# Edge loop of a graph layer: one head of the values weighed by ScalarE, and the softmax's maximum and sum taken into the exponential

## The chip, the cores and the metric

The kernel runs on one core of a Trainium2 chip. The metric is the device time of one execution in microseconds (us). Before the change three runs gave 2769.37, 2779.38 and 2781.32 us, with a median of 2779.38. Engines are named as in the profile: PE (TensorE, matmuls; PEld is its weight load), DVE (VectorE), ACT (ScalarE), POOL (GpSimd) and SP (SyncE, which issues DMAs). Each engine works through its own queue in order; engines wait for one another by semaphores.

## The reference, cut to what matters

There are 3125 nodes with 256 features and 103125 directed edges (each node has a self-loop). A graph layer, a linear-attention mixer and a mixture of experts follow one another. The change is in the graph layer, in the attention over edges. With `H = 4` heads of `DK = 56`:

```python
att = jnp.einsum('ehd,ed->eh', k, q.sum(axis=1)) / SQRT_DK
v = jnp.concatenate([Vn, ek], axis=1).reshape(-1, H, DK)

def seg_softmax(att, idx, n):
    m = jax.ops.segment_max(att, idx, num_segments=n)
    e = jnp.exp(att - m[idx])
    s = jax.ops.segment_sum(e, idx, num_segments=n)
    return e / (s[idx] + 1e-16)

res = (v * att[:, :, None]).reshape(-1, H * DK)
agg = jax.ops.segment_sum(res, col, num_segments=n) + jax.ops.segment_sum(res_i, row, num_segments=n)
```

It is computed for both directions of every edge. A node's value is 192 features of its own (three heads of 56 and 24 features of the fourth head) followed by 32 features made of the edge's time.

## The kernel before, in words

The nodes are sorted by their number of edges and cut into 25 blocks of 128 nodes, one node to a partition. A block has as many *slots* as its busiest node has edges: 60 in the first block that is worked on, then 44, 42, 40 and so on down to 22, 854 in all. The work is cut further into 118 *chunks* of six to eight slots. All blocks with their chunks are worked on in `edge_blocks` (L1203 to L1491), in an order that is written out by hand (`tc.manual_schedule`, L1435); nothing is reordered by a planner. The loop over the chunks `q` issues, on every engine's queue in this order:

- `gather(q + 3)`: POOL fetches one row of the node table per slot (L357).
- `first_times(q)`: PE adds up one group of time features (L1340).
- `take` (L1417) on ACT, for the block that ended three chunks ago.
- If the chunk before was the last of its block ("over"), `softmax_exp` of that block: ACT's exponential (L1376), all eight columns (two directions, four heads) at once.
- `find(q + 1)`: DVE picks each slot's record (L1305, L1306) and forms part of the logits (L1310, L1311). It needs `compare(q + 1)`.
- `angles(q + 1)`: PE transposes the times that find left (L1317, tile pt); ACT copies them out (L1319, tile turned, called lT in the code) and copies the gathered values into the tile keep (L1322); then ACT runs `compare(q + 2)` (one L1295 per slot, and L1296); then PE multiplies by the frequencies (L1326) and ACT takes sines and squares, three times (L1328, L1329).
- If over: `softmax_two` of that block on DVE (L1382 to L1392: sum, reciprocal, scaling, and the two directions added into the tile both), and then `weigh` for each of its chunks. In weigh DVE multiplies three heads of the values by their weights (L1400), the 24 features of the fourth (L1402) and the time features (L1404), and PE adds the slots up in PSUM with one matmul by the identity per slot (L1406, two passes each in float32).
- `logits(q)` on DVE (L1349 to L1357), which needs the sines and squares of `angles(q)`.
- `finish` for a block that ended three chunks ago, and at the end of a block `sums` and `softmax_one` (L1412 to L1414 and L1363 to L1372: add the parts, take the maximum over the slots, subtract it).

Two consequences of in-order queues matter. On PE, the transpose of `angles(q + 2)` stands behind the whole burst of L1406 that a block boundary issues. On ACT, `compare(q + 3)` stands behind the copy of that transpose. The tile keep has nine buffers; the gathered rows have four.

A second path for other graphs (`edge_tiles`, called at L858) is skipped at run time unless a check of the fast path fails.

Of the kernel before, what the change touches and what calls it, by code (L numbers as in the profile page):

```python
# [10 lines left out]
F32 = mybir.dt.float32  # L11
I32 = mybir.dt.int32
AF = mybir.ActivationFunctionType
OP = mybir.AluOpType
AX = mybir.AxisListType
# [3 lines left out]
P = 128  # L19
D = 256  # L20
TD = 32
GH = 4
DK = (D - TD) // GH
# [43 lines left out]
def bc(ap, axis, n):  # L67

    u = ap.unsqueeze(axis)
    shape = list(u.shape)  # L70
    shape[axis] = n
    return u.to_broadcast(shape)
# [1130 lines left out]
def edge_blocks(tc, a, table, kept, abuf, slots, ordt, ord_i, counts, bad, ident, ones, scatter_rows, gather_rows,  # L1203
# [7 lines left out]
    nc = tc.nc  # L1211
# [3 lines left out]
    line = list(reversed(range(len(slots))))  # L1215
    for i in line:
        c = slots[i]
        k = -(-c // CHUNK)
# [3 lines left out]
    with ExitStack() as ctx:  # L1222
        one = ctx.enter_context(tc.tile_pool(name="e1", bufs=1))
        two = ctx.enter_context(tc.tile_pool(name="e2", bufs=2))
# [12 lines left out]
        for dst, k in ((w3, "w_time"), (b3, "b_time")):  # L1237
            s = a[f"L0_gnn_{k}"]
# [21 lines left out]
        blk, chk = {}, {}  # L1260
# [99 lines left out]
        def softmax_one(i):  # L1360
            c, b = slots[i], blk[i]
            att, shared = b["att"], b["shared"]
            nc.vector.tensor_tensor(shared[:, :c], shared[:, :c], bc(b["k"][:, :, 2], 2, GH), OP.add)  # L1363
            ah = att[:, :c, :6].rearrange("p s (d h) -> p s d h", d=2)
            nc.vector.tensor_tensor(ah, ah, bc(shared[:, :c, :3], 2, 2), OP.add)
            nc.vector.scalar_tensor_tensor(att[:, :c, 6:], att[:, :c, 6:], -2.0, bc(shared[:, :c, 3], 2, 2),
                                           op0=OP.mult, op1=OP.add)

            mx = two.tile([P, 2 * GH], F32, name="mx")
            nc.vector.tensor_reduce(mx, att[:, :c].rearrange("p s k -> p k s"), AX.X, OP.max)  # L1370
            nc.vector.tensor_scalar(mx, mx, 0.1 * NEG, None, op0=OP.max)
            nc.vector.tensor_tensor(att[:, :c], att[:, :c], bc(mx, 1, c), OP.subtract)  # L1372

        def softmax_exp(i):
            af = blk[i]["att"][:, :slots[i]]
            nc.scalar.activation(af, af, AF.Exp, scale=scale)  # L1376

        def softmax_two(i):
            c, b = slots[i], blk[i]
            att = b["att"]  # L1380
            sm = b["sm"] = two.tile([P, 2 * GH], F32, name="sm")
            nc.vector.tensor_reduce(sm, att[:, :c].rearrange("p s k -> p k s"), AX.X, OP.add)  # L1382
            rc = two.tile([P, 2 * GH], F32, name="rc")
            nc.vector.tensor_scalar(rc, sm, 1e-16, None, op0=OP.add)
            nc.vector.reciprocal(rc, rc)
            nc.vector.tensor_tensor(att[:, :c], att[:, :c], bc(rc, 1, c), OP.mult)
            both = b["both"] = two.tile([P, CAP, GH], F32, name="both")
            nc.vector.tensor_tensor(both[:, :c, :3], att[:, :c, :3], att[:, :c, 3:6], OP.add)
            nc.vector.tensor_tensor(both[:, :c, 3], att[:, :c, 6], att[:, :c, 7], OP.add)

            nc.vector.tensor_tensor(sm, sm, rc, OP.mult)
            nc.vector.tensor_tensor(sm[:, 6:7], sm[:, 6:7], sm[:, 7:], OP.add)  # L1392

        def weigh(q):
            i, s0, s1 = chunks[q]
            n, c, b, keep = s1 - s0, slots[i], chk[q]["b"], chk[q]["keep"]
            if s0 == 0:
                b["pa"] = psa.tile([P, KEEP], F32, name="pa")
            v3 = keep[:, :n, :3 * DK].rearrange("p s (h e) -> p s h e", e=DK)
            nc.vector.tensor_tensor(v3, v3, bc(b["both"][:, s0:s1, :3], 3, DK), OP.mult)  # L1400
            v1 = keep[:, :n, 3 * DK:PROJ]
            nc.vector.tensor_tensor(v1, v1, bc(b["both"][:, s0:s1, 3], 2, TAILH), OP.mult)  # L1402
            vt = keep[:, :n, PROJ:].rearrange("p s (m j) -> p s m j", j=TD)
            nc.vector.tensor_tensor(vt, vt, bc(b["att"][:, s0:s1, 6:], 3, TD), OP.mult)  # L1404
            for s in range(n):
                nc.tensor.matmul(b["pa"], ident, keep[:, s, :], start=(s0 + s == 0), stop=(s0 + s == c - 1))  # L1406
# [24 lines left out]
        n = len(chunks)  # L1431
# [3 lines left out]
        with tc.manual_schedule():  # L1435
# [8 lines left out]
            for q in range(n):  # L1444
                i, s0, s1 = chunks[q]
# [6 lines left out]
                if over is not None:  # L1452
                    softmax_exp(over)
# [3 lines left out]
                if over is not None:  # L1457
                    softmax_two(over)
                    j0 = q - len(pieces[over])
                    for j in range(j0, q):  # L1460
                        weigh(j)
# [3 lines left out]
                if ends[q] is not None:  # L1465
                    sums(i)
                    softmax_one(i)
# [7 lines left out]
                if q == 4:  # L1475
                    between()
            softmax_exp(line[-1])
            for q in (n - 3, n - 2):
                if ends.get(q) is not None:
                    take(ends[q])  # L1480
                    finish(ends[q])
            softmax_two(line[-1])
            for j in range(n - len(pieces[line[-1]]), n):
                weigh(j)
# [172 lines left out]
```

## Time and profile before

| what | value |
|---|---|
| runs | 2769.37, 2779.38, 2781.32 us, median 2779.38 |
| profiled execution | 2770.56 us, its span 2768.9 us |
| mean granted TensorE clock | 0.703 of full speed |
| busy over the span | DVE 2089.2 us (75%), PE 1951.6 (70%), POOL 1485.0 (54%), ACT 1226.2 (44%) |
| block boundaries, 663 to 2106 us of the span | 1443 us: DVE 1406.8 busy, PE 1108.6, POOL 950.3, ACT 854.0 |
| what comes before and after the edge loop | 0 to 540 us: preparation and mixer; 2135 to 2769 us: the rest of the layer and the experts |

The three runs have a median 8.8 us above the profiled execution. The times between the first and the last instruction are the span; sums of durations below are set against the profiled execution. In lists by group the columns are: line, engine, operation, tiles, shapes and count; then busy us and mean ns of one; then the engine's idle time before these instructions, with what ended it. In a list of waits: who waited for whom, us in total, times, longest. In a timeline: start in us, length in us, engine, line, operation, count, and in brackets the idle time before it with what ended it. Matmuls are pipelined, so that a busy PE is not PE at its peak.

### The profile page before, as it was taken

The numbers are of one execution on the slowest core, as the hardware profiler recorded it, in microseconds if no ns is written. First come the engines' busy times: TensorE is split into PE (matmuls) and PEld (weight loads), VectorE is DVE, ScalarE is ACT, GpSimd is POOL, SyncE is SP. The second block draws the span as 40 slices with busy tenths as digits, with TensorE's granted clock in tenths as the row PEclk, the third lists the DMA queues.
The fourth block names the chain that finished last, engine by engine and source line by source line (L and its number), as shares of the span: only waits on it lengthen the run. The fifth ranks groups of instructions, "written<-read, shape, count | busy, mean of one in ns | idle before, by whom it ended". The sixth has DMA issues, their size and how long they took to land. (4 is left out here: it accounts for less than half of the span.)

```text
span 2768.9 us, 25919 instructions
## 1 busy us (share of the span) xinstructions
PE 1951.6 (70%) x6193; PEld 1210.2 (44%) x6193; DVE 2089.2 (75%) x3744; ACT 1226.2 (44%) x3019; POOL 1485.0 (54%) x1527
## 2 busy tenths in 40 slices
PE   1138567558777777777777778777775945499994
PEld 0014234424344444444544434444544633277773
DVE  5545667669999999999999999999995557122226
ACT  1101122355655556655566666566562333033332
POOL 2632665476767776666666777666560541522220
PEclk7559778856666666666666666766756865599997
DMA  9541563496766666655566666566563762355554
GB/s 284 190 125 52 185 202 117 150 383 193 204 179 183 182 185 183 190 171 167 167 180 191 193 191 182 171 182 191 152 191 124 254 194 86 130 169 175 171 162 143
DMA packets 233243, 493.03 MB, mean 178 GB/s; under 512 B 33573, under 2 KB 144452, under 8 KB 232452
## 3 DMA queue, kind: packets, MB, share of 16 engines
q0 software_dynamic: 88720, 327.84, 39.1%
q1 hardware_dynamic: 114916, 130.10, 15.0%
q10 hardware_dynamic: 29456, 33.42, 3.8%
q8 instruction: 54, 0.88, 0.1%
q14 instruction: 97, 0.79, 0.1%
HBM read 412.86 MB, written 78.37 MB: 177 GB/s over the span
## 5 line engine op out<-in xcount | busy, mean ns | idle before, releaser
L357 POOL DMA_INDIRECT rowt<-table,idx x854 | 971.8, 1138 | 466.4 <-issue 433.2
L1326 PE MATMUL ps_u<-wide,turned 49*128 49x448 f32 (+2 forms) x708 | 532.3, 913 | 43.5 <-ACT turned L1319 40.8
L1406 PE MATMUL pa<-keep,ident 128*128 128x256 f32 x1708 | 428.6, 418 | 17.9 <-DVE keep L1404 17.7
L1406 PEld LDWEIGHTS pa<-keep,ident 128*128 128x128 f32 x1708 | 360.6, 213 | 110.5 <-DVE keep L1404 39.9
L1340 PE MATMUL pe<-te,ident 128*128 128x256 f32 x472 | 202.3, 577 | 245.0 <-ACT te L1329 243.0
L1326 PEld LDWEIGHTS ps_u<-wide,turned 49*128 49x128 f32 x708 | 196.2, 296 | 285.3 <-issue 186.1
L1340 PEld LDWEIGHTS pe<-te,ident 128*128 128x128 f32 x472 | 128.6, 297 | 381.0 <-ACT te L1329 361.7
L1319 ACT COPY turned<-pt 42x128 f32<-42x128 f32 (+2 forms) x118 | 30.6, 259 | 571.5 <-PE pt L1317 571.5
L1357 DVE TENSOR_REDUCE att<-rowt 128x56 f32<-128x1792 f32 (+2 forms) x118 | 245.8, 2083 | 4.0
L1295 ACT ACTIVATE rowt<-rowt,KT 128x60 f32<-128x60 f32 x854 | 215.8, 334 | 17.6 <-DMA rowt<-table,idx 17.4
L1305 DVE TENSOR_TENSOR rowt<-rowt 128x1260 f32<-128x1260 f32 (+2 forms) x118 | 178.2, 1510 | 40.3 <-DMA rowt<-table,idx 25.5
L1354 DVE TENSOR_TENSOR rowt<-rowt,qq 128x672 f32<-128x672 f32 (+2 forms) x236 | 197.6, 878 | 4.0
L1129 ACT ACTIVATE hT<-ps_h,b 128x128 f32<-128x128 f32 x256 | 94.1, 368 | 236.3 <-PE ps_h L1128 236.1
L351 POOL DMA_INDIRECT ybuf<-y,to_i x64 | 61.5, 960 | 242.6 <-DVE y L1137 228.9
L1328 ACT ACTIVATE half<-ps_u 128x448 f32<-128x448 f32 (+2 forms) x354 | 190.8, 539 | 0.3
L1128 PE MATMUL ps_h<-zT,w 128*128 128x128 f32 x1024 | 179.9, 295 | 12.4 <-ACT hT L1129 9.9
L1306 DVE TENSOR_REDUCE KT<-rowt 128x21 f32<-128x1260 f32 (+2 forms) x118 | 178.3, 1511 | 4.1
L1128 PEld LDWEIGHTS ps_h<-zT,w 128*128 128x128 f32 x1024 | 150.1, 192 | 57.0 <-ACT hT L1129 44.8
L1400 DVE TENSOR_TENSOR keep<-keep,both 128x1176 f32<-128x1176 f32 (+2 forms) x118 | 167.0, 1416 | 0.0
L1322 ACT COPY keep<-rowt 128x1344 f32<-128x1344 f32 (+2 forms) x118 | 159.2, 1349 | 10.8 <-PE pa L1406 10.8
L1133 PE MATMUL ps_e<-w,hT 128*128 x512 | 157.4, 390 | 0.0
L722 PE MATMUL ps<-w,xT 128*128 x172 | 99.6, 716 | 63.5 <-ACT xT L286 63.5
(369 smaller groups left out, 3250.6 us busy)
## 6 DMA issues: line engine op xcount, KB each, us to landing
w<-in_L_ffn_w_dram SPq DMA_DIRECT2D x80, 512.0 KB, 3.6
rowt<-table,idx POOLq DMA_INDIRECT x854, 4.1
h<-in_L_gnn_Wa_dram SPq DMA_DIRECT2D x19, 512.0 KB, 4.4
zbuf<-zero SPq DMA_DIRECT2D x1, 8514.0 KB
zr<-zbuf SPq DMA_DIRECT2D x64, 129.0 KB
yb<-ybuf SPq DMA_DIRECT2D x16, 384.0 KB, 5.5
xbuf<-blank SPq DMA_DIRECT2D x1, 5654.0 KB
abuf<-zero SPq DMA_DIRECT2D x1, 5632.0 KB
```

The lines of the kernel that those rows point to most:

```text
L357: nc.gpsimd.indirect_dma_start(out=dst, out_offset=None, in_=buf[:, :], in_offset=IndirectOffsetOnAxis(ap=idx, axis=0))
L1128: nc.tensor.matmul(ps[:, f, :], w1[:, c, f * P:(f + 1) * P], zT[:, c, :], start=(c == 0), stop=(c == 1))
L1295: nc.scalar.activation(key[:, s, :], key[:, s, :], AF.Square, bias=chk[q]["b"]["k"][:, s0 + s, 1:2])
L1305: nc.vector.tensor_tensor(times, times, bc(rowt[:, :n, :CAP], 2, 3), OP.mult)
L1306: nc.vector.tensor_reduce(b["times"][:, s0:s1, 1::2], times, AX.X, OP.add)
L1326: nc.tensor.matmul(ps[:, :n * 2 * TD], lT, wide[:, k, :n * 2 * TD], start=True, stop=True)
L1328: nc.scalar.activation(half[:, :n, :].rearrange("p s j -> p (s j)"), ps[:, :n * 2 * TD], AF.Sin)
L1340: nc.tensor.matmul(pe[:, :e - s, :], ident, chk[q]["te"][:, 0, s:e, :], start=(s0 + s == 0), stop=(s0 + e == c))
L1354: nc.vector.tensor_tensor(to, kt, bc(qq[:, :n, d, :], 2, 3), OP.mult)
L1357: nc.vector.tensor_reduce(b["att"][:, s0:s1, :], rowt[:, :n, :8 * TD].rearrange("p s (k j) -> p s k j", j=TD), AX.X, OP.add)
L1400: nc.vector.tensor_tensor(v3, v3, bc(b["both"][:, s0:s1, :3], 3, DK), OP.mult)
L1406: nc.tensor.matmul(b["pa"], ident, keep[:, s, :], start=(s0 + s == 0), stop=(s0 + s == c - 1))
```

## The change

Three things are changed, all in `edge_blocks`.

1. `softmax_one` no longer subtracts the maximum from the logits. It computes `low = -scale * maximum`, eight numbers per node.
2. `softmax_exp` runs one exponential per column (eight instead of one), with that column of `low` as bias, and has each deliver the sum over the slots as by-product into `sm`. `softmax_two` no longer computes the sum.
3. In `weigh`, for every block but the first, ACT multiplies the first head's 56 features slot by slot, with the weight as a scale per partition; DVE multiplies the second and third head only. The first block is weighed by DVE as before.

```diff
@@ softmax_one
             nc.vector.tensor_scalar(mx, mx, 0.1 * NEG, None, op0=OP.max)
-            nc.vector.tensor_tensor(att[:, :c], att[:, :c], bc(mx, 1, c), OP.subtract)
+            b["low"] = two.tile([P, 2 * GH], F32, name="low")
+            nc.vector.tensor_scalar(b["low"], mx, -scale, None, op0=OP.mult)
 
         def softmax_exp(i):
-            af = blk[i]["att"][:, :slots[i]]
-            nc.scalar.activation(af, af, AF.Exp, scale=scale)
+            b = blk[i]
+            sm = b["sm"] = two.tile([P, 2 * GH], F32, name="sm")
+            for k in range(2 * GH):
+                ak = b["att"][:, :slots[i], k]
+                nc.scalar.activation(ak, ak, AF.Exp, scale=scale, bias=b["low"][:, k:k + 1], accum_out=sm[:, k:k + 1])
 
         def softmax_two(i):
             c, b = slots[i], blk[i]
             att = b["att"]
-            sm = b["sm"] = two.tile([P, 2 * GH], F32, name="sm")
-            nc.vector.tensor_reduce(sm, att[:, :c].rearrange("p s k -> p k s"), AX.X, OP.add)
+            sm = b["sm"]
             rc = two.tile([P, 2 * GH], F32, name="rc")
@@ weigh
-            v3 = keep[:, :n, :3 * DK].rearrange("p s (h e) -> p s h e", e=DK)
-            nc.vector.tensor_tensor(v3, v3, bc(b["both"][:, s0:s1, :3], 3, DK), OP.mult)
+
+            h0 = 0 if i == line[0] else 1
+            for s in range(n * h0):
+                nc.scalar.activation(keep[:, s, :DK], keep[:, s, :DK], AF.Copy, scale=b["both"][:, s0 + s, 0:1])
+            vh = keep[:, :n, h0 * DK:3 * DK].rearrange("p s (h e) -> p s h e", e=DK)
+            nc.vector.tensor_tensor(vh, vh, bc(b["both"][:, s0:s1, h0:3], 3, DK), OP.mult)
```

Each matmul of weigh waits for the copy of its own slot. DVE's multiplications wait for none of the copies. The copies stand in ACT's queue behind `angles(q + 1)`, where weigh stands in the order above; the matmuls and their order are unchanged.

## The prediction

> **What bounds the kernel now.** First the windows view, cut at the edge loop, then its waits, then one block boundary in order of time. Its columns are busy us of PE, PEld, DVE, ACT, POOL, then the granted clock:
>
> ```profile
> 663.00:2106.00 1443.00, 1108.63 (x2863) 661.64 (x2863) 1406.80 (x1799) 854.04 (x2005) 950.33 (x817) 0.65 0.61 177
> ```
>
> VectorE is busy for 1406.8 of 1443 us, ScalarE for 854.0. By shares alone VectorE is the limit, and work taken from it is time won. The waits of the same stretch say more:
>
> ```profile
> ACT turned L1319 <- PE pt L1317: 550.2, 109, 19.1
> DVE rowt L1305 <- ACT rowt L1296: 5.0, 9, 1.2
> PE pa L1406 <- DVE keep L1404: 5.8, 14, 1.0
> ```
>
> ScalarE's idle time is one wait, for the transpose of L1317, up to 19.1 us at once; and VectorE's few stalls end with ScalarE's L1296. The boundary after the 40-slot block shows how they hang together (lines of the timeline):
>
> ```profile
> 896.41 0.47 ACT L1376 ACTIVATE att<-att 128x320 f32<-128x320 f32 x1
> ...
> 899.78 0.26 ACT L1319 COPY turned<-pt 48x128 f32<-48x128 f32 x1 [2.90 <-PE pt L1317]
> ...
> 903.63 0.16 DVE L1392 TENSOR_TENSOR sm<-sm 128x1 f32<-128x1 f32 x1
> ...
> 906.18 19.81 PE L1406 MATMUL pa<-keep,ident 128*128 128x256 f32 x80 [0.60 <-DVE keep L1404]
> ...
> 908.36 0.63 ACT L1329 ACTIVATE te<-half 128x512 f32<-128x512 f32 x1
> ...
> 926.69 0.27 PE L1317 MATMUL pt<-ident,KT 128*48 128x128 f32 x1
> 927.00 0.26 ACT L1319 COPY turned<-pt 48x128 f32<-48x128 f32 x1 [18.00 <-PE pt L1317]
> ...
> 931.16 0.19 ACT L1296 ACTIVATION_READ_ACCUMULATOR rowt<-rowt,ones 128x1 f32 x1
> ...
> 931.38 1.66 DVE L1305 TENSOR_TENSOR rowt<-rowt 128x1440 f32<-128x1440 f32 x1 [0.62 <-ACT rowt L1296]
> ```
>
> softmax_two ends at 903.8. VectorE's first weighed chunk starts PE's burst for the block (80 passes for 40 slots, 906.2 to 926.0). The next transpose is queued behind the burst (926.7); ScalarE's lT copy waits for it (927.0); compare is queued behind that copy on ScalarE and ends at 931.35; find, two chunks on, starts at 931.38. So between 903 and 931 two chains run side by side, VectorE's own work and PE's burst with its followers, and they arrive together. Same reading for the 22 inner boundaries (second to twenty-third block): find starts a mean of 0.35 us after compare's end; in 13 of them within 0.06 us, most of these with a marked stall. There is no slack for PE to start late.
>
> **The change, part by part.** Rows (groups by shape):
>
> ```profile
> L1400 DVE TENSOR_TENSOR keep<-keep,both 128x1176 f32<-128x1176 f32 x68 | 93.4, 1374 | 0.0
> ...
> L1400 DVE TENSOR_TENSOR keep<-keep,both 128x1344 f32<-128x1344 f32 x39 | 60.4, 1549 | 0.0
> ```
>
> ```profile
> L1295 ACT ACTIVATE rowt<-rowt,KT 128x60 f32<-128x60 f32 x824 | 207.4, 334 | 4.2 <-DMA rowt<-table,idx 4.0
> ...
> L1296 ACT ACTIVATION_READ_ACCUMULATOR rowt<-rowt,ones 128x1 f32 x114 | 21.3, 186 | 0.0
> ```
>
> *VectorE's removals.* 168 elements more cost 1549 - 1374 = 175 ns, 1.042 ns each. The slots number 854; all but the first block's 60 lose 56 elements: 794 x 56 x 1.042 = 46.3 us. The 25 sums (L1382, median 620 ns) go: 15.5 us. The 25 subtractions (L1372, median 434) become a multiply of 8 elements (222, as L1371): 5.3 us. Together 67.1 us of VectorE.
>
> *ScalarE's weighing.* 794 new instructions of 56 elements; nearest is L1295 (60 elements, one pointer operand): 334 ns, and eight in a row took 1.99 us, a pitch of (1.99 - 0.33) / 7 = 0.237. So 794 x 0.237 = 188 us of ScalarE time. The Trainium skill, "ScalarE: Activation LUTs", section "Rules for kernel authors", speaks against this: multiplications belong on VectorE. By the rows the price per slot is 237 ns instead of 58; if ScalarE's time were the path this would be 794 x 0.179 = +142 us. The 550 us of idle in front of L1319 hide the throughput: 40 x 0.237 = 9.5 us fits into this boundary's 18.0. I put 0 for throughput; the cost is in the order, next.
>
> *The wait that appears.* The copies stand in ScalarE's queue behind all of angles of the next chunk, whose last Square ends at 908.99, after softmax_two (903.79). Each matmul of L1406 waits for its own slot's copy, so the burst starts at 908.99 + 0.33 = 9.32 instead of 6.18: 3.14 us late. VectorE does not wait for the copies. After that PE is slower (19.8 / 40 = 0.495 us a slot) than the copies (0.237), so the burst keeps its length. Behind the copies (done by 918.8) stands only the next lT, which waits for PE anyway; no DMA is issued or moved by the change. Everything behind the burst (transpose, lT, compare) is 3.14 later, and compare ends at 934.5. VectorE, with 5 x 0.467 + 0.72 + 0.2 = 3.3 us less to do, is there at 930.76 - 3.3 = 927.5 and waits 7 us. So its savings in this stretch buy nothing, and the delay is paid in full. The same reading, "end of the last L1329 + 0.33 - start of L1406", over the 22 inner boundaries:
>
> ```
> late  3.0 3.4 3.1 3.5 3.5 3.2 3.3 3.3 3.3 3.3 3.2 3.3 4.3 3.7 3.7 3.5 3.5 3.4 3.5 3.5 3.4 3.2  sum 74.9
> spare 0.0 0.2 0.0 0.1 0.0 0.0 0.0 0.0 0.0 0.0 0.0 0.0 1.8 1.5 0.2 0.7 0.7 0.0 1.2 0.6 0.0 0.0  sum  7.0
> ```
>
> "Spare" is find's start less compare's end, less the 0.03 of a bare handover. Net +67.9. From find on, both kernels do the same in the same order, so each boundary's delay stays.
>
> *The multiply for the subtraction* starts find, and with it the transpose, about 0.2 us earlier: -0.2 x 22 = -4.4.
>
> *Eight exponentials.* Eight of c elements, each with a sum; L1376's rows give 0.85 ns per element, so 334 - 24 x 0.85 = 314 ns at c = 36. In the accumulating L1296 the read starts 0.60 into a 0.69 instruction and the next one 0.09 after the read: an exponential with its sum has a pitch of about its own duration, 8 x 0.314 = 2.5 us against 0.45 now, +2.1. They lie in ScalarE's wait for the transpose after L1376, 2.2 to 3.4 us (2.90 above), so 0. softmax_two has find in front of it and is not late either. If each read cost its full 186 ns, eight take 4.0 us and angles ends up to 1.2 us later, 1.0 as a mean: upper end +22. The 32-byte stride of the input has no row; I take the dense one.
>
> *PE's clock.* PE's pause before the burst grows from 0.6 to 3.7 us. The Trainium skill, "TensorE: Matmul & The Clock Gate", section "HAM oscillation — how this bites in real kernels", warns against pauses above about 3.4 us, since the clock falls to half; by that alone a boundary would pay a fresh warm-up of some 3.4 us at half speed, an estimate of 1.7 us each, +37 in all. The rows say most of it is paid already: the granted clock is 0.50 before each burst and for its first 4.2 us (mean of 12 bursts in slices of 1 us). The last block's burst starts after 11.88 us of pause and stays at 0.50 for 5.2 us:
>
> ```profile
> 2117.00:2118.00 1.00, 1.00 (x4) 0.80 (x3) 1.00 (x3) 0.00 (x0) 0.00 (x0) 0.50 1.01 426
> 2118.00:2119.00 1.00, 1.00 (x4) 0.82 (x3) 0.17 (x1) 0.00 (x0) 0.00 (x0) 0.50 0.99 412
> 2119.00:2120.00 1.00, 1.00 (x5) 0.83 (x5) 0.00 (x0) 0.00 (x0) 0.00 (x0) 0.93 0.96 401
> ```
>
> One more cold us costs half a us: between 0 and 22 x 0.54 = +12. I take the middle, +6.
>
> *A wait on every matmul*, already met, has no row on PE; VectorE's event instructions at L1305 last 50 ns at the median, so 0 to 750 x 0.05 = +37. I take 0: TensorE issues ahead during a 190 ns weight load.
>
> *The ends.* First block: all on VectorE, softmax_two 1.2 earlier, and so the burst: -1.2. Twenty-fourth: burst 3.6 late, and the time features that the last logits need, 1.0 before their use now, end 2.6 late. Last block: exponentials 2.1 longer and nothing beside them, the sum (0.47), the subtraction and part of a chunk's weighing gone: +1.0. Together +2.4.
>
> Sum: 67.9 - 4.4 + 0 + 6 + 0 + 2.4 = +72 on the profiled execution's 2770.6: 2843. The runs shown (2769 to 2781) have a mean 6 us above it, their median 9; I add 6: **2849**, +2.5%. Measured differences below 0.5% (14 us) tell nothing from no change.
>
> **The rivals.**
> *VectorE stays the limit* and the savings come out: -67, 2703 profiled. For it: 97% busy. It needs boundaries where VectorE arrives last; it decides where PE's burst starts less than 0.35 us late, which would take angles to end 3 us earlier than it does. If only the start of the burst were as before, just the 0.9 us that softmax_two gains would count: -20.
> *The delay is absorbed*: the burst shrinks, because a longer queue of ready slots or an earlier warm clock helps it, by as much as it starts late: no change, 2771 profiled. Against it: PE is busy without a gap in the burst now.
> *More than the start is late*: reads at full price, waits on each matmul, clock by the upper end: 72 + 22 + 37 + 6 = +137, 2908 profiled.
> *ScalarE's throughput as the limit*: 854 + 188 + 25 x 2.1 = 1095 of 1443 us; it has room, so no case of its own.
>
> **How the numbers follow.** Main case 0.68; the heavier one 0.13; partly absorbed, +0.5 to +1.3%, 0.06; absorbed, within 0.5%, 0.05; VectorE's savings win 0.08. So faster 0.08, same 0.05, slower 0.87. The range leaves out the faster and absorbed cases and the top of the heavy one: 2805 (under half of the delay) to 2890 (main sum plus reads and the rest of the clock, 2849 + 22 + 6, and a third of the waits).
>
> **What would show it.** Right: L1305 stalls 6 to 7 us once per block on ScalarE's compare, VectorE idle in the loop up by about 140 us, its busy time down 67; PE's first matmul of a block waits for ScalarE, 3 us after the last Square; exponentials end before the transpose arrives. Wrong: bursts that start within 1 us of the first chunk, or are shorter; no long stall before L1305. A wait for L1380 before lT shows the exponentials dearer than put.

## The result: 2.35% slower, and the profile after

Four runs of the changed kernel gave a median of 2837.07 us (2833.0 to 2843.37), four of the kernel before beside them 2774.5 (2769.37 to 2781.32). The ratio is 1.0235, with a 95% interval of 1.021 to 1.026. The time lies in the predicted range, 12 us under the predicted 2849.

From the page after the change, the busy times and three of the costliest groups (idle time with its releaser at the end):

```profile
PE 1952.1 (69%) x6193; PEld 1209.8 (43%) x6193; DVE 2025.5 (71%) x3719; ACT 1469.7 (52%) x4188; POOL 1447.8 (51%) x1527
...
L1413 PE MATMUL pa<-keep,ident 128*128 128x256 f32 x1708 | 426.1, 416 | 91.9 <-ACT keep L1405 82.0
...
L1305 DVE TENSOR_TENSOR rowt<-rowt 128x1260 f32<-128x1260 f32 (+2 forms) x118 | 178.6, 1513 | 165.6 <-ACT rowt L1296 107.4
...
L1405 ACT ACTIVATE keep<-keep,both 128x56 f32<-128x56 f32 x794 | 186.5, 326 | 1.1 <-DVE both L1391 1.1
```

VectorE did lose its work: 2089.2 to 2025.5 us busy. But it stands 165.6 us in front of find's first instruction (40.3 before), and the burst's matmuls now wait for ScalarE's copies, 82 us, where they waited 17.9 in all. The boundary of the 40-slot block again, in order of time (start, length; the first line is the last of its eight exponentials):

```profile
899.08 0.35 ACT L1380 ACTIVATE att<-att,low 128x40 f32<-128x40 f32 x1
...
900.62 0.26 ACT L1319 COPY turned<-pt 48x128 f32<-48x128 f32 x1 [1.10 <-PE pt L1317]
...
903.40 0.16 DVE L1395 TENSOR_TENSOR sm<-sm 128x1 f32<-128x1 f32 x1
...
909.20 0.63 ACT L1329 ACTIVATE te<-half 128x512 f32<-128x512 f32 x1
...
909.74 9.38 ACT L1405 ACTIVATE keep<-keep,both 128x56 f32<-128x56 f32 x40
...
910.12 20.06 PE L1413 MATMUL pa<-keep,ident 128*128 128x256 f32 x80 [3.70 <-ACT keep L1405]
...
930.88 0.27 PE L1317 MATMUL pt<-ident,KT 128*48 128x128 f32 x1
931.19 0.26 ACT L1319 COPY turned<-pt 48x128 f32<-48x128 f32 x1 [12.07 <-PE pt L1317]
...
935.35 0.19 ACT L1296 ACTIVATION_READ_ACCUMULATOR rowt<-rowt,ones 128x1 f32 x1
...
935.56 1.66 DVE L1305 TENSOR_TENSOR rowt<-rowt 128x1440 f32<-128x1440 f32 x1 [7.37 <-ACT rowt L1296]
```

softmax_two ends at 903.6. PE's burst starts at 910.1, 6.6 us later; before it was 2.4. The 40 copies end at 919.1, long before the burst does (930.2), and the burst is as long as before (20.06 against 19.81). The transpose follows the burst's end by 0.7 us and compare ends 4.35 us after the lT copy's start, both as before; so the whole shift goes through to find, and VectorE waits 7.37 us for it.

All 22 inner boundaries, read in this way from both traces:

```
mean over 22 boundaries                        before    after
burst starts after the last Square, us          -3.08     0.28
burst starts after softmax_two, us               2.13     6.10
sum of the burst lengths, us                    375.5    374.4
sum of VectorE's stalls at that find, us          5.5    127.1
```

At seven of the 22 stalls after the change the profile names a gather's DMA as releaser and not compare; but at every one of the 22 find starts 0.03 us after compare's end.

From the first block's exponential to the twenty-fourth's the time grew from 1410.4 to 1474.0 us: -1.5 in the first block and +65.1 in the 22 others, 3.0 each.

### The profile page after: what moved, and what is told of

It is laid out like the page before. It is cut to its first block, busy times and chain, and to the rows that moved or that the text cites. A ratio compares the mean times of both kernels' runs of the same rounds, so it can differ in the third digit from the quotient of the medians.

```text
span 2841.6 us, 27167 instructions
## 1 busy us (share of the span) xinstructions
PE 1952.1 (69%) x6193; PEld 1209.8 (43%) x6193; DVE 2025.5 (71%) x3719; ACT 1469.7 (52%) x4188; POOL 1447.8 (51%) x1527
## 5 line engine op out<-in xcount | busy, mean ns | idle before, releaser
L357 POOL DMA_INDIRECT rowt<-table,idx x854 | 931.7, 1091 | 448.7 <-issue 250.4
L1305 DVE TENSOR_TENSOR rowt<-rowt 128x1260 f32<-128x1260 f32 (+2 forms) x118 | 178.6, 1513 | 165.6 <-ACT rowt L1296 107.4
L1405 ACT ACTIVATE keep<-keep,both 128x56 f32<-128x56 f32 x794 | 186.5, 326 | 1.1 <-DVE both L1391 1.1
```

The source lines that it names most:

```text
L357: nc.gpsimd.indirect_dma_start(out=dst, out_offset=None, in_=buf[:, :], in_offset=IndirectOffsetOnAxis(ap=idx, axis=0))
L1305: nc.vector.tensor_tensor(times, times, bc(rowt[:, :n, :CAP], 2, 3), OP.mult)
L1405: nc.scalar.activation(keep[:, s, :DK], keep[:, s, :DK], AF.Copy, scale=b["both"][:, s0 + s, 0:1])
```

## The experiments

The theories on record: A, the burst starts late since its first matmul waits for a copy that is queued behind angles; B, the time that 794 copies take of ScalarE, or a wait on every matmul; C, the eight exponentials. Later D, that a late start always costs its three us.

The kernel before itself took different times on the chips used: a median of 2776 us beside the first four experiments (the weighing alone, one copy, unread copies, first chunk by VectorE), 2837 beside the next four, 2818 beside the last four. Each ratio is against the kernel before on the same chip. The kernel before has one trace, from a run of 2770.56 us; the eight traces from the two slower chips have gaps that the last section describes. Where these bear on a reading, the edge loop of the trace, from the first block's exponential to the twenty-fourth's, is set beside the kernel before's 1410.4 us as well.

**The weighing alone**, with the softmax as before:

```diff
 # kernel before, weigh()
-v3 = keep[:, :n, :3 * DK].rearrange("p s (h e) -> p s h e", e=DK)
-nc.vector.tensor_tensor(v3, v3, bc(b["both"][:, s0:s1, :3], 3, DK), OP.mult)
+h0 = 0 if i == line[0] else 1
+for s in range(n * h0):
+    nc.scalar.activation(keep[:, s, :DK], keep[:, s, :DK], AF.Copy, scale=b["both"][:, s0 + s, 0:1])
+vh = keep[:, :n, h0 * DK:3 * DK].rearrange("p s (h e) -> p s h e", e=DK)
+nc.vector.tensor_tensor(vh, vh, bc(b["both"][:, s0:s1, h0:3], 3, DK), OP.mult)
```

> The weighing by ScalarE alone; the softmax as before the change. Theory A (late start: the first matmul of each block's burst waits for a copy that stands behind all of angles): the burst starts 0.3 us after the last Square, as in the changed kernel, and the time is that of the changed kernel within 10 us (+55 to +70 us over before). Rival B (the time that 794 copies take of ScalarE, or a wait on every matmul): the same, so this run does not tell A from B. Rival C (the eight exponentials and their reads are what costs): about as before, within 15 us.

Measured: 2837.99 us against 2775.97, ratio 1.0219 (1.0166 to 1.0271). The burst starts 0.28 us after the last Square. Over the 22 inner boundaries its trace is 66.1 us longer than the kernel before's (65.1 with the whole change). The weighing carries the whole loss; C falls as its cause.

**One copy per block.** ScalarE weighs the first slot of each block only:

```diff
 # changed kernel, weigh()
-h0 = 0 if i == line[0] else 1
-for s in range(n * h0):
-    nc.scalar.activation(keep[:, s, :DK], keep[:, s, :DK], AF.Copy, scale=b["both"][:, s0 + s, 0:1])
-vh = keep[:, :n, h0 * DK:3 * DK].rearrange("p s (h e) -> p s h e", e=DK)
-nc.vector.tensor_tensor(vh, vh, bc(b["both"][:, s0:s1, h0:3], 3, DK), OP.mult)
+h0 = 0 if i == line[0] or s0 else 1
+if h0:
+    nc.scalar.activation(keep[:, 0, :DK], keep[:, 0, :DK], AF.Copy, scale=b["both"][:, s0, 0:1])
+    vh = keep[:, :1, DK:3 * DK].rearrange("p s (h e) -> p s h e", e=DK)
+    nc.vector.tensor_tensor(vh, vh, bc(b["both"][:, :1, 1:3], 3, DK), OP.mult)
+vh = keep[:, h0:n, :3 * DK].rearrange("p s (h e) -> p s h e", e=DK)
+nc.vector.tensor_tensor(vh, vh, bc(b["both"][:, s0 + h0:s1, :3], 3, DK), OP.mult)
```

> The changed kernel, but ScalarE weighs only one slot of each block, the first (24 copies instead of 794); VectorE weighs all the others with all three heads and pays one short instruction per block more. Theory A: one copy behind angles delays the burst as much as all: burst starts 0.3 us after the last Square, +50 to +70 us over before, as in the changed kernel. Rival B: 24 of 794 copies, so -20 to +5 us. Rival C: +60 us; this run does not tell A from C, the run with the weighing alone does.

Measured: 2846.64 us, ratio 1.025 (1.0201 to 1.03). Two of its waits between 663 and 2120 us (us in total, times, longest):

```profile
PE pa L1415 <- ACT keep L1405: 78.1, 22, 3.9
...
DVE rowt L1305 <- ACT rowt L1296: 76.3, 20, 5.2
```

24 copies cost as much as 794: the same 3.9 us at most on PE, once per block. What counts is that a copy is there, not how many. B falls.

**Copies that nobody reads**, 794 of them at the same place, added to the kernel before:

```diff
 # kernel before, weigh()
+if i != line[0]:
+    junk = two.tile([P, CHUNK, DK], F32, name="junk")
+    for s in range(n):
+        nc.scalar.activation(junk[:, s, :], ones[:, :DK], AF.Copy, scale=b["both"][:, s0 + s, 0:1])
 v3 = keep[:, :n, :3 * DK].rearrange("p s (h e) -> p s h e", e=DK)
```

> The kernel before, with 794 added ScalarE instructions of 56 elements at the same place in its queue and with the same pointer operand, into a tile that nothing reads (added work; nothing is left out). Theory A: PE does not wait for them and they end before PE's next transpose: 0 to +5 us. Rival B, as far as it is ScalarE's time: +40 us or more. Rival C: nothing said.

Measured: 2772.9 us, ratio 0.9989 (0.9972 to 1.0006). The added group in its trace, and what find waits:

```profile
L1402 ACT ACTIVATE junk<-ones,both 128x56 f32<-128x56 f32 x794 | 186.5, 326 | 1.6 <-DVE both L1388 1.6
```

```profile
DVE rowt L1305 <- ACT rowt L1296: 7.7, 7, 3.5
```

The same 186.5 us of ScalarE as in the changed kernel, at no measurable cost: they lie in its wait for the transpose, as the prediction's zero said.

**First chunk by VectorE**, the other chunks as in the changed kernel:

```diff
 # changed kernel, weigh()
-h0 = 0 if i == line[0] else 1
+h0 = 0 if i == line[0] or s0 == 0 else 1
```

> The changed kernel, but the first chunk of every block is weighed by VectorE with all three heads; ScalarE weighs the other chunks (some 630 copies instead of 794). Theory A: PE starts when VectorE has done the first chunk, some 2.3 us after softmax_two, and PE's six us on that chunk at half clock cover the wait for the first copy; the delay is gone and the earlier softmax_two remains: 15 to 25 us faster than before (2750 to 2760). Rival B: four fifths of the loss stay, +45 to +55 us. Rival C: the loss stays, +60 us.

Measured: 2753.82 us, ratio 0.9926 (0.9901 to 0.9951), 22 us faster than before. Its boundary of the 40-slot block:

```profile
899.17 0.16 DVE L1395 TENSOR_TENSOR sm<-sm 128x1 f32<-128x1 f32 x1
...
902.12 18.86 PE L1413 MATMUL pa<-keep,ident 128*128 128x256 f32 x80
...
904.98 0.63 ACT L1329 ACTIVATE te<-half 128x512 f32<-128x512 f32 x1
905.51 7.52 ACT L1405 ACTIVATE keep<-keep,both 128x56 f32<-128x56 f32 x32
...
926.37 1.71 DVE L1305 TENSOR_TENSOR rowt<-rowt 128x1440 f32<-128x1440 f32 x1 [1.94 <-ACT rowt L1296]
```

The burst starts 2.8 us after softmax_two, ahead of the last Square, and the copies come in time for the second chunk. One line of code turns +62 into -22 us. The prediction had put -20 for a burst that starts as before. And yet VectorE still stalls on compare (1.94 here, 37.8 us in all between 663 and 2120 us): its savings do not come out, since the burst in front of the transpose is as long as ever (373.7 us over the 22 boundaries, 375.5 before).

**The softmax part alone**, twice:

```diff
 # changed kernel, weigh() as before the change; softmax_one, softmax_exp, softmax_two as changed
-h0 = 0 if i == line[0] else 1
-for s in range(n * h0):
-    nc.scalar.activation(keep[:, s, :DK], keep[:, s, :DK], AF.Copy, scale=b["both"][:, s0 + s, 0:1])
-vh = keep[:, :n, h0 * DK:3 * DK].rearrange("p s (h e) -> p s h e", e=DK)
-nc.vector.tensor_tensor(vh, vh, bc(b["both"][:, s0:s1, h0:3], 3, DK), OP.mult)
+v3 = keep[:, :n, :3 * DK].rearrange("p s (h e) -> p s h e", e=DK)
+nc.vector.tensor_tensor(v3, v3, bc(b["both"][:, s0:s1, :3], 3, DK), OP.mult)
```

> The softmax part of the change alone; VectorE weighs everything as before. Theory A: the eight exponentials (2.9 us instead of 0.5 in the changed kernel's trace) hide in ScalarE's wait for the transpose; softmax_two and with it the burst come 0.9 us earlier at each block: 15 to 25 us faster than before. Rival C (dear exponentials): +30 us or more. As VectorE and the burst's chain gain the same 0.9 us, stalls before find stay as they were, 10 to 20 us in all.

> The same kernel as the earlier run of the softmax part alone, which came out 1.1% slower beside a kernel before that itself took 60 us longer on that chip; there ScalarE stood 58 us in gaps of about one us between instructions that nothing in the trace explains. On a chip without such gaps theory A says as before: burst and softmax_two 0.9 us earlier per block, 15 to 25 us faster than the kernel before. Rival C (the exponentials cost by themselves): +20 us or more, without those gaps.

Measured: 2864.96 us against 2837.09, ratio 1.0107 (1.0053 to 1.0161), and then 2828.46 against 2818.4, ratio 1.0038 (1.0019 to 1.0056). Both missed what A expected, and both chips had gaps. In the second trace, at the 34-slot block (idle time in brackets; "issue" is time in which the engine waited for nothing that the profile shows):

```profile
1440.48 0.34 ACT L1380 ACTIVATE att<-att,low 128x34 f32<-128x34 f32 x1
...
1440.99 0.20 ACT L1380 ACTIVATION_READ_ACCUMULATOR att<-att,low 128x1 f32 x1 [0.17 <-issue]
...
1442.39 0.26 ACT L1319 COPY turned<-pt 42x128 f32<-42x128 f32 x1 [1.20 <-issue]
1443.10 1.31 ACT L1322 COPY keep<-rowt 128x1344 f32<-128x1344 f32 x1 [0.46 <-issue]
```

Six blocks of the second run have nearly no such gaps (under 0.8 us on ScalarE and PE together); from exponential to exponential they are 0.4 us shorter each than in the kernel before's trace, five such blocks of the first run 0.8 shorter. That has the sign of A's 0.9, but it compares traces of different chips; and whether the longer row of ScalarE instructions draws more gaps was not tried. What this part costs or gains as a whole stays open.

**The burst cut in two**: the second half of a block's chunks is weighed one chunk later, behind the next transpose. The same edit was made to the changed kernel, to the kernel before, and to the changed kernel with the first chunk by VectorE.

```diff
 # loop over the chunks, rest = None before it
-    for j in range(j0, q):
+    half = (j0 + q) // 2
+    for j in range(j0, half):
         weigh(j)
+elif rest is not None:
+    for j in range(*rest):
+        weigh(j)
+    rest = None
+if over is not None:
+    rest = (half, q)
 logits(q)
```

> The changed kernel, but a block's burst is cut in two: the first half of its chunks is weighed where it was, the second half one chunk later, after the next transpose has been put into PE's queue. Theory A, second part (what holds find back is a burst in front of the transpose, so that VectorE's savings come out only where the chain has room): with half a burst before the transpose, the late start costs little; find's stalls fall under 20 us in all and VectorE's 67 us come out for the most part: 40 to 70 us faster than before. Rival B (ScalarE's time or the waits of the matmuls): 20 us faster at most. Rival D (VectorE's work doesn't matter, only the start does): +40 us or more, the start is as late as in the changed kernel.

> The kernel before with the same cut of the burst. Theory A: VectorE is then the only limit and was almost the only one already; its stalls before find are some 8 us on ScalarE: 5 to 12 us faster than before. If the cut itself were what pays, it would be 40 us or more.

> Both: the burst cut in two, and the first chunk of each block weighed by VectorE alone. Theory A: the chain has the most room; VectorE is the limit with 67 - 9 = 58 us less to do: 55 to 65 us faster than before, find's stalls under 10 us in all. Compared with the cut alone it loses the 9 us of VectorE and gains what stalls were left there. Rival B: about half of that gain.

Measured: the changed kernel with the cut 2932.15 us, ratio 1.0335 (1.0277 to 1.0392); the kernel before with the cut 2811.83, 0.9913 (0.9886 to 0.9941); the cut with the first chunk by VectorE 2843.15, 1.0025 (1.0001 to 1.0048). The first and the third missed widely, and by more than gaps: in the first one, the ten blocks without them (under 0.8 us) are 4.0 us longer each than the kernel before's. The second gained 25 us where 5 to 12 were expected; its edge loop is 9 us shorter than the kernel before's 1410.4. Four of the first one's waits between 663 and 2120 us say why it lost:

```profile
PE pa L1413 <- ACT keep L1405: 182.4, 41, 8.2
...
ACT ag L1424 <- PE pa L1413: 145.1, 21, 8.8
...
DVE rowt L1305 <- ACT rowt L1296: 83.5, 22, 4.5
...
DVE ag L1430 <- ACT ag L1424: 68.3, 17, 6.5
```

The second half's copies now stand behind angles of the next chunk, so the burst starts late twice (41 waits); its end is late for take, which is a ScalarE instruction ahead of all that follows; and finish on VectorE waits for take. It is the same mistake as in the change under study. The third, which also has its second half's copies there, shows the same waits for copies (115.5 us on PE, 29 times, between 663 and 2150 us).

So in the last version all of a block's copies stay where they were, and only VectorE's and PE's part of the second half moves; an odd number of chunks is now cut with the larger part first. The lines for the last block are left out here:

```diff
 # changed kernel with the cut; copies(j) is the loop of ScalarE's instructions taken out of weigh(j)
-    half = (j0 + q) // 2
+    half = (j0 + q + 1) // 2
+    for j in range(j0, q):
+        copies(j)
     for j in range(j0, half):
         weigh(j)
```

> The same without the first chunk's exception: ScalarE weighs one head of every slot, the burst starts 0.3 us after the last Square and is late by 3.3 us, but only half a burst stands in front of the next transpose. Theory A (it is not the lateness as such, but that it reaches find): 60 to 80 us faster than before, in spite of the late start. Rival D (a late start always costs its 3 us per block): 0 to 10 us faster.

> Everything in the kernel changed, with two differences: the first chunk of each block is weighed by VectorE alone, and the second half of a block's chunks is multiplied by VectorE and summed by PE one chunk later (ScalarE's copies for all chunks are issued at once, where they were). Theory A: neither the start of the burst nor its length in front of the next transpose holds find back; VectorE's 67 us less 9 us come out, and its stalls of the kernel before too: 60 to 75 us faster than before. Rival B (ScalarE's time): under 30 us faster.

> The kernel before with the burst cut in two, again, for the same reason. Theory A: what the chain cost VectorE in the kernel before was its stalls in front of find, some 16 us by the trace: 8 to 25 us faster than before.

Measured, on one chip: this cut 2780.88 us against 2818.4, ratio 0.9868 (0.9813 to 0.9923); with the first chunk by VectorE 2762.71, 0.9818 (0.976 to 0.9875); the kernel before with the cut of the earlier runs, again, 2802.98, 0.9942 (0.9915 to 0.9968). The version with both is the fastest of the three, 56 us under the kernel before. What find mainly waits for in its trace, between 663 and 2120 us:

```profile
DVE rowt L1305 <- DMA rowt<-table,idx: 5.4, 8, 2.5
DVE rowt L1305 <- ACT rowt L1296: 4.6, 2, 3.5
```

Of the 37.8 us of stalls on ScalarE without the cut, 4.6 are left. VectorE's savings come out once the chain in front of find has room: at the 22 boundaries find starts a mean of 4.0 us after compare's end here, and the cut alone gives 15 us, with ScalarE's help 56. The start still late but only half a burst in front of the transpose (first of the three) gives 38, so D falls in its strict form: lateness costs where it reaches find, and there it still costs (find 0.4 us after compare's end as a mean, 23 us of stalls on ScalarE in that trace).

The sizes are less sure than the order, since the kernel before has no trace from this chip. The edge loops of the version with both, of the one with the late start and of the cut alone are 38, 25 and 10 us shorter than the kernel before's 1410.4, with their gaps counted in, so at least that is not the chip. Seven blocks of the version with both have nearly no gaps and are 2.2 us shorter each; VectorE's savings without the first chunks, 67 - 9 = 58 us, would be 2.4 for each of 24 blocks. Against what was expected, it fell 4 us short of the lower end, the one with the late start 22 us.

## Why the prediction was right, point by point

- *Two chains arrive together at find, and PE's is the one without room.* Right: the kernel before stalled 5.5 us at those 22 finds, the changed one 127.1; VectorE's idle time from the first exponential to the last burst's end grew by 128 us (about 140 put). The run with the first chunk by VectorE, in which the burst starts as early as before, shows that the loss hangs on that start.
- *Burst at the last Square + 0.33, 3.4 us late as a mean, 67.9 net of the spare.* It starts 0.28 after the last Square, 3.36 later than before against that mark. With the -4.4 for the earlier find, 63.5 were put for the 22 boundaries without the clock; 65.1 came. The fit is closer than its parts, by luck: the weighing alone cost 66.1 where 67.9 was put, so that the softmax part is left with -1.0 where -4.4 was put. Why the earlier find gave so little was not looked into.
- *Throughput of the copies 0.* Right: 186.5 us busy (188 put), and unread they cost nothing measurable.
- *Exponentials hidden.* Right in the end, with nothing to spare: eight and their reads last 2.90 us at 40 slots against 0.47 before, +2.4 where +2.1 was put, and ScalarE's wait behind them shrank from 2.90 to 1.10 there, to less than 0.1 in three of the 22. The term mis-sized is the duration: 355 ns each at 40 slots, not 317.
- *PE's clock +6.* This step failed: it measured 0. The bursts are as long as before (374.4 against 375.5), although PE's pause before them grew from a mean of 0.23 to 3.55 us. The clock in the two traces says why. It stands at 0.50 throughout the 3 us before every one of the 22 bursts, before and after, so the longer pause takes nothing away. From a burst's start it stays there for a mean of 4.4 us before (3.1 to 6.1) and 4.3 after (2.9 to 6.1). The one row from which the upper end came, 5.2 us after 11.9 us of pause, lies within that scatter; in the changed kernel the same burst had 3.5 us after 9.8. The 37 us estimated for a whole warm-up per boundary had nothing to be paid on either.
- *A wait on every matmul 0.* Right, by the same sums.
- *The ends +2.4.* The first block gave -1.5 (-1.2 put). From the twenty-fourth block's exponential to the last burst's end it was +0.7 where +3.6 was put: of the burst's late start there only about 0.1 reached the next block's exponential.
- *VectorE's 67 us.* The three groups lost 46.1 (167.0 to 120.9), 15.8 and 5.5, together 67.4. They only lengthened its stalls.
- *The sum.* -1.5 + 65.1 + 0.7 = 64.3 us in the edge loop; the medians differ by 62.6. The profiled execution's span is 72.7 longer; 8 of it lie in stages that the change doesn't touch. Of the 12 us between forecast and result 6 are the clock's and some 3 the ends'; some 2 more come from the 6 added to go from the profiled execution to the runs, whose median before is now 4 above it, and what is left is within the spread of the runs.

The rival that VectorE's savings decide was refuted in the form given, and is true behind it: they are worth having once the chain is relieved.

## What to carry to other kernels

Before a busy engine is relieved, ask what its consumer's first instruction will wait for: an idle engine's free time counts only at the place in its queue where the work is put, and one instruction there can cost as much as eight hundred. Read slack where two chains meet (here "find's start less compare's end", a mean of 0.35 us before the change), not from busy shares. A helper engine can be given everything but the first piece, as here: the first chunk stays with the engine that is there in time, and covers the helper's arrival.

## What was not expected of the hardware

The kernel before took 2776, 2837 and 2818 us as the median of 20 to 36 runs on three chips. In all eight traces from the two slower chips ScalarE and PE stand in gaps, often of about a microsecond, in front of plain instructions, with nothing named by the profile. Gaps over 0.25 us on ScalarE come to 33 to 75 us in the edge loop, 75 and 47 us in the two traces of the softmax part alone; none of the traces from the fastest chip, nor the two of the change itself, has any there. They are not of the loop only: the stages ahead of it and behind it, which no run changes, take 27 to 54 us longer in these eight traces than in the kernel before's. In both runs of the softmax part the disturbed blocks that lost the most are largely the same (the first, third, eleventh and twelfth among them), which speaks for a place in the program. The loading of instructions doesn't show as the cause: the profile has 65 such transfers in the edge loop of the kernel before's trace and 65 to 73 in four of the traces with gaps, and only 7 to 15 of the 63 to 108 gaps of each overlap one. The cause is open.

A second finding is that a pause of PE cost nothing where the clock was low already: at 0.50 before every burst in both traces, it took as long to rise after pauses of 3.55 us as after 0.23 us, as means. The boundary of the 40-slot block in slices of 1 us, three before the change (the burst starts at 906.18) and three after it (910.12); PE's busy time is the first number behind the comma, the granted clock the third from the end:

```profile
905.00:906.00 1.00, 0.57 (x1) 0.00 (x0) 1.00 (x3) 0.99 (x2) 1.00 (x1) 0.50 0.56 220
...
909.00:910.00 1.00, 1.00 (x4) 0.81 (x3) 1.00 (x2) 0.00 (x0) 1.00 (x1) 0.50 0.84 180
910.00:911.00 1.00, 1.00 (x4) 0.78 (x4) 1.00 (x3) 0.00 (x0) 0.75 (x1) 0.59 0.34 140
```

```profile
908.00:909.00 1.00, 0.00 (x0) 0.00 (x0) 1.00 (x3) 0.97 (x3) 1.00 (x1) 0.50 0.83 205
...
914.00:915.00 1.00, 1.00 (x4) 0.73 (x4) 1.00 (x2) 1.00 (x6) 0.00 (x0) 0.50 0.00 0
915.00:916.00 1.00, 1.00 (x6) 0.89 (x5) 0.97 (x3) 1.00 (x5) 0.00 (x0) 0.87 0.00 0
```
